# Two-directional Mamba blocks on one core: the output projection one unit later, the eleventh unit's exponentials ahead of a copy, and an earlier load of GpSimd's B

## The chip, the cores and the metric

The kernel runs on one core of one Trainium2 chip. The metric is the device time of one launch in microseconds (us). Three runs of the kernel before gave 26886.77, 26917.85 and 26921.99 us, median 26917.85 us. One further execution was profiled; it took 26881.74 us.

The engines are named as in the profile: PE (TensorE, matmuls), DVE (VectorE), ACT (ScalarE), POOL (GpSimd) and SP (SyncE, which here only issues DMAs, in the order of the program). Every engine works through its own queue in order; between engines there are semaphores.

## The reference, cut to what matters

An image of 64 channels and 128 x 128 pixels is read as sequences, once along its rows and once along its columns. Each sequence goes through a Mamba block forward and backward. A group normalisation and a residual follow, then a block of two 3x3 convolutions with batch normalisation, which is of no concern here.

```python
def mamba(seq, p):                    # seq: (sequences, 128, 64)
    xz = einsum('blc,ec->ble', seq, in_w)
    x, z = xz[..., :128], xz[..., 128:]
    x = silu(causal_conv(x, conv_w, conv_b))          # u
    xdbl = einsum('bld,ed->ble', x, xp_w)
    dt, Bm, Cm = split(xdbl, (4, 16, 16))
    delta = softplus(einsum('blr,dr->bld', dt, dt_w) + dt_b)
    A = -exp(A_log)                                   # (128, 16)
    # scan over tokens t, state h of 128 x 16 for each sequence:
    #   h = exp(delta_t * A) * h + (delta_t * u_t) * B_t ;  y_t = sum_n h * C_t
    y = selective_scan(x, delta, A, Bm, Cm, D)        # + u * D
    y = y * silu(z)
    return einsum('bld,cd->blc', y, out_w)
xr = 0.5 * (mamba(rows) + flip(mamba(flip(rows))))    # the same for columns with other weights
x_rec = 0.5 * (xr + xc); x = silu(group_norm(x_rec)) + x
```

All arithmetic is float32. There are 8 images, 2 orientations, 128 sequences each and 2 directions.

## The kernel before, in words

**Chunks and units.** A chunk `g` is 4 sequences of 128 tokens (512 columns) of one image and one orientation: 32 row chunks and 32 column chunks an image, 512 chunks in all. The scan of a chunk has 128 channels x 16 states x 2 directions; one *unit* is half of the channels (64 channels as 2 x 32) x 4 states of one direction, laid on 128 partitions x 1024 columns. A chunk has 16 units, whose order stands in `ORDER` as (group of 4 states, direction, kind); even units are half 0, odd units half 1.

**What a unit takes.** `decay` makes exp(delta A): two ACT instructions. `drive` multiplies delta u with B: on DVE with B in PSUM (`pb`, made by one matmul in `b_rows` for two units) for kind V, on GpSimd with B loaded by DMA (`bt`, `b_tile`) for kind G. For kind T the product with B is made on tokens: ACT writes `X` = duT * BT in `spread` (four instructions a call, eight calls a chunk), PE turns it in `turn`. `scan` is one DVE instruction, `weigh` one GpSimd multiplication with C (`c`, loaded by DMA in `c_rows`), and `add_up` sums over the states on PE, four units later. In the text a unit's number is written behind the step: `decay(11)`, `drive(13)`, `scan(7)`. Decays of V and G units write the PSUM tile dA0 or dA1, one buffer each, so `decay(k)` waits for the scan two units back that read the same tile.

**The order.** Everything is written out by hand (`tc.manual_schedule`): a loop over `s`, with chunk `n` and unit `r`, issues in each unit the B of later units, the next unit's decay and drive, this unit's scan and weighing, one step of the generator `prepare` for the next chunk, the sums of unit `s - 4`, and DMA issues. `prepare` makes the next chunk's u, delta and their copies during this chunk: a step in each unit. The steps that matter here, as they were:

- r = 8: softplus on ACT (line 307), which needs a table load before it; line 420 loads the exponentials' table back after it.
- r = 9: `bp` (B and C) on PE; `du` = delta u on DVE (326); on ACT the copy `dl` of delta (328) and two small edge copies (330); then `keep(1, du)` and `keep(0, dl)`, 4 DMAs each to a DRAM scratch `dd` (314).
- r = 10: `decay(11)` on ACT, `bc` copy (335) and its DMA to `bd` (337), four transposes `dt` on PE of `du` into the second half of the tile `op` (343), `replicate(g, 0, 0)`: two DMAs of 512 KB that read `dd` back, each row four times, into the next chunk's dl and du for half 0; `add_up(6)`; the DMA c0; at the end of the unit the output projection `emit` of the *previous* chunk into the first half of `op` (487, and 492 for columns).
- r = 11: `b_rows(13)` (409), `turn(12)`, the copy `duT` (347), `replicate(g, 1, 0)` (half 1: `dl10`, `du10`), the DMA `b2` of GpSimd's B, and ACT's copies out of `op` (500 or 505).
- r = 12: `btp` on PE (353). r = 13: its copy `BT` (359), `replicate(g, 1, 1)`, the first `spread`; one further spread in each of the units 14, 15, 0 to 4.
- r = 15 and 0: `drive(0)` and `drive(1)` of the next chunk, which need du of half 0 and `du10`; GpSimd's `drive(2)` needs `b2`.

`dp`, `op`, `btp` and the convolution's `cps` share one PSUM tile (tag `pt`), so each waits until its predecessor was read: `dt` waits for the copy `dl`, which reads delta from `dp`.

Chunks come in three sorts for this text: **row** chunks, where `emit` is one matmul; **normalising** row chunks (the first 16 or so of the following image's), in which one piece of the finished image is normalised in each chunk on ACT, GpSimd and SP; **column** chunks, where `emit` has a second matmul that adds the rows' result, two copies and a `bn_stats`.

Of the kernel before, what the change touches and what calls it, by code (L numbers as in the profile page):

```python
# [46 lines left out]
def tile_mamba2d_then_resblock(ctx: ExitStack, tc: tile.TileContext, x, par, gn, p_w, o_w, new_p, bn, cst, out):  # L47
# [171 lines left out]
    with ExitStack() as st:  # L219
# [54 lines left out]
        def prepare(g, before):  # L274


            w = wt[g["o"]]
            yield
            zp = psa.tile([P, N], F32, name="zp", tag="b")
            nc.tensor.matmul(  # L280
                zp.rearrange("p (q t) -> p q t", t=W), w["wz"], g["xs"][0:C, :, PAD : PAD + W], start=True, stop=True
            )
            yield
            g["sz"] = work.tile([P, N], F32, name="sz", bufs=3)
            nc.scalar.copy(g["sz"], zp)
            cp = psm.tile([P, 2, N], F32, name="cp", tag="pt")
            for d in range(2):
                for k in range(2):
                    t = PAD - 2 * k if d == 0 else PAD + 2 * k + 1
                    nc.tensor.matmul(  # L290
                        cp[:, d, :].rearrange("p (q t) -> p q t", t=W), w["wc"][:, d, k, :],
                        g["xs"][:, :, t : t + W], start=k == 0, stop=k == 1,
                    )
                yield
            yield
            u = work.tile([P, 2, N], F32, name="u")
            nc.scalar.activation(u, cp, AF.Silu, bias=w["conv_b"])  # L297
            if before is not None:
                nc.scalar.activation(before["sz"], before["sz"], AF.Silu)
            g["u"] = u  # L300
            yield
            dp = psm.tile([P, 2, N], F32, name="dp", tag="pt")
            for d in range(2):
                nc.tensor.matmul(dp[:, d, :], w["wd"], u[:, d, :], start=True, stop=True)  # L304
            yield
            yield
            nc.scalar.activation(dp, dp, AF.Softplus, bias=w["dt_b"])
            yield
            dd = g["dd"] = scratch.tile([2, 2, 32, NQ, N], F32, name="dd")

            def keep(k, v):

                for q in range(NQ):
                    nc.sync.dma_start(
                        out=dd[k, :, :, q, :].rearrange("d c t -> c d t"), in_=v[32 * q : 32 * (q + 1)]
                    )


            bp = psa.tile([P, N], F32, name="bp", tag="b")
            for d in range(2):  # L320
                nc.tensor.matmul(
                    bp[2 * NS * d : 2 * NS * (d + 1), :], w["wbc"], u[:, d, :], start=True, stop=True,
                    skip_group_check=True,
                )
            du = work.tile([P, 2, N], F32, name="du", tag="nat")
            nc.vector.tensor_mul(du, dp, u)
            dl = work.tile([P, 2, N], F32, name="dl", tag="nat")
            nc.scalar.copy(dl, dp)  # L328
            for d, edge in enumerate((0, W - 1)):
                nc.scalar.copy(dl[:, d, :].rearrange("p (s t) -> p s t", t=W)[:, :, edge], far)  # L330
            keep(1, du)
            keep(0, dl)
            yield
            bc = work.tile([4 * NS, N], F32, name="bc", tag="tok", bufs=3)
            nc.scalar.copy(bc, bp[0 : 4 * NS, :])
            bd = scratch.tile([2 * NS, 2, N], F32, name="bd")
            nc.sync.dma_start(out=bd.rearrange("n d t -> d n t"), in_=bc)
            g["bd"] = bd

            dt = (shared.pop("pt", None) or psm.tile([P, 2, N], F32, name="dt", tag="pt"))[:, 1, :]  # L340
            for q in range(SEQ):
                c = slice(W * q, W * (q + 1))
                nc.tensor.transpose(dt[:, c], du[:, TD, c], ident)  # L343
            replicate(g, 0, 0)
            yield
            g["duT"] = work.tile([P, SEQ, P], F32, name="duT", bufs=1)
            nc.scalar.copy(g["duT"].rearrange("p q c -> p (q c)"), dt)  # L347
            replicate(g, 1, 0)
            yield

            bt = psm.tile([P, 2, N], F32, name="btp", tag="pt")[:, 0, 0 : 8 * SEQ]
            for q in range(SEQ):
                nc.tensor.matmul(
                    bt[:, 8 * q : 8 * (q + 1)], u[:, TD, W * q : W * (q + 1)], w["wbc"][:, 4 * TG : 4 * TG + 8],
                    start=True, stop=True,
                )
            yield
            g["BT"] = work.tile([P, 8 * SEQ], F32, name="BT", bufs=1)
            nc.scalar.copy(g["BT"], bt)
            replicate(g, 1, 1)  # L360
            yield
            yield
            replicate(g, 0, 1)
            yield

        def spread(g, ng, q):

            t = g["X", ng, q] = work.tile([P, P, 4], F32, name="X", bufs=8)
            for n in range(4):
                k = 8 * q + 4 * (ng - TG) + n  # L370
                nc.scalar.activation(  # L371
                    t[:, :, n], g["duT"][:, q, :], AF.Copy, scale=g["BT"][:, k : k + 1]
                )

        def replicate(g, half, d):

            for k, what in enumerate(("dl", "du")):
                t = rep.tile([P, 2, N], F32, name=what, bufs=5)
                src = g["dd"][k, d, :, 2 * half : 2 * half + 2, :].rearrange("c q t -> c (q t)")
                nc.sync.dma_start(  # L380
                    out=t.rearrange("p q t -> p (q t)"), in_=src.unsqueeze(1).to_broadcast([32, 4, 2 * N])
                )
                g[what, half, d] = t
# [85 lines left out]
        def add_up(g, r):  # L469

            for half in range(2):
                s = g.pop(("s", r + half))
                for j in range(2):
                    q = 2 * half + j
                    nc.tensor.matmul(  # L475
                        g["yp"][32 * q : 32 * (q + 1), :], fold, s[:, j, :], start=False, stop=r == UN - 2,
                        skip_group_check=True,
                    )
# [73 lines left out]
        def conv1(b):  # L552
# [29 lines left out]
        PER = 2 * NCH  # L582
# [4 lines left out]

        EARLY = {3: 4, 4: 7, 11: 12, 12: 15}

        SPREAD = {13: (2, 0), 14: (2, 1), 15: (2, 2), 0: (2, 3), 1: (3, 0), 2: (3, 1), 3: (3, 2), 4: (3, 3)}  # L590

        AHEAD = {15: 3, 0: 3, 7: 3, 8: 3}

        ROWS = {14: 0, 3: 5, 6: 8, 11: 13}

        FETCH = {
            10: ["c0"], 11: ["b2"], 12: ["c2"], 14: ["c4"], 15: ["c5"], 2: ["c8"], 3: ["b10"], 4: ["c10"],
            6: ["c12"], 8: ["c13"],
        }
        blocks, shared = {}, {}  # L600
# [12 lines left out]
        with tc.manual_schedule():  # L613
# [3 lines left out]
                pass  # L617
            for r in (10, 11, 12, 14, 15):
                fetch(gs[0], r)
            for r in (13, 14, 15):  # L620
                spread(gs[0], *SPREAD[r])
            b_rows(*at(0))
            decay(*at(0))
            drive(*at(0))
# [1 line left out]
            for s in range(total + UN):  # L626
# [9 lines left out]
                    if n + 2 < len(gs):  # L636
                        columns(gs[n + 2])
                kind = ORDER[(r + 1) % UN][2]
                if r in ROWS and (g := after if r >= 14 else this):
                    b_rows(g, ROWS[r])  # L640
                if kind == "T" and live:
                    turn(*at(s + 1))
                if kind != "T" and s + 1 < total:
                    decay(*at(s + 1))
                if r in EARLY and live:
                    decay(this, EARLY[r])
# [8 lines left out]
                    gate(prev)  # L655
                if s == total - 1:
                    nc.scalar.activation(this["sz"], this["sz"], AF.Silu)
                if r in CONV and n % PER > 6 or r >= CONV[0] and n % PER == 6:
                    next(conv3, None)
                op = None  # L660
                if r == OUT and (prev or after):
                    op = shared["pt"] = psm.tile([P, 2, N], F32, name="op", tag="pt")
                next(pieces, None)
                if r in SPREAD and (g := after if r >= 13 else this):
                    spread(g, *SPREAD[r])
                if r == LAG and live:
                    skip(this)
                if s % 2 == 0 and LAG <= s < total + LAG:
                    add_up(*at(s - LAG))
                if r in NORM and n % PER:  # L670
                    next(norm, None)
                if g := after if r >= 10 else this:
# [4 lines left out]
                    stack(gs[n + 2], n + 2)  # L677
                if r == 4 and NCH - 6 <= n % PER < PER - 6:
                    load_columns(n // PER, *divmod(n % PER - NCH + 6, 4))
                if r == OUT and prev:  # L680
                    output = emit(prev, op[:, 0, :])
                    next(output)
                elif r == OUT + 1:
                    next(output, None)
                elif r == OUT + 2:
                    next(output, None)
                elif r == OUT + 3 and n % PER == 0 and prev:
                    for _ in conv3:
                        pass
                    norm = normalize(prev["b"], stats.pop(prev["b"]))  # L690
                    next(norm)
                    conv3 = conv1(prev["b"])
# [152 lines left out]
```

## Time and profile before

| | us |
|---|---|
| median of 3 runs | 26917.85 |
| profiled execution | 26881.74 |
| its span (first to last instruction) | 26880.0 |
| first scan at, last scan ends at | 126.2, 25761.4 |
| DVE busy | 23985.6 (89%) |
| GpSimd busy | 23978.1 (89%) |
| ACT busy | 22417.1 (83%) |
| PE busy (matmul) | 19283.9 (72%) |
| mean DMA rate | 171 GB/s |
| granted TensorE clock | 0.839 |

The profiled execution lies 0.13% under the median. The 512 chunks take 25635 us of the span, 50.1 us each; behind them come the second convolution and the last pass. By durations a chunk's 16 scans, 8 drives, `du` and gating are 47.4 us on DVE (neighbours overlap by some 0.08 us each in the records, so about 46 us in sequence); 16 weighings of 2.34 us and 4 drives of 2.36 us are 46.9 us on GpSimd. No engine is busy throughout; the idle time sits at a few places of the chunk.

### The profile page before, as it was taken

How to read it: one execution, taken by the hardware profiler on the slowest of the kernel's cores; microseconds unless marked ns; L12 is line 12 of the kernel's file. 1: busy time of each engine (PE TensorE's matmuls, PEld its weight loads, DVE VectorE, ACT ScalarE, POOL GpSimd, SP SyncE). 2: the span in 40 equal slices, each digit the busy share in tenths (PEclk: the TensorE clock that was granted, in tenths of full speed). 3: DMA queues.
4: the chain of work that ended last, by engine and by line, in shares of the span. 5: the costliest groups of instructions: out<-in, count | busy, mean ns of one | idle time of the engine just before them, and what ended most of it. 6: DMA issues, size and time to landing. Idle time of an engine off the chain costs nothing. (4 is left out here: it accounts for less than half of the span.)

```text
span 26880.0 us, 268089 instructions
## 1 busy us (share of the span) xinstructions
PE 19283.9 (72%) x75308; PEld 7512.1 (28%) x75308; DVE 23985.6 (89%) x14093; ACT 22417.1 (83%) x41390; POOL 23978.1 (89%) x10404
## 2 busy tenths in 40 slices
PE   5667777777777777777776777777777777777776
PEld 2222222222322223222232222222222222322232
DVE  8999999999999999999999999998999999999942
ACT  7888888888888888888888888888888888888842
POOL 7999999999999999999999999999999999999930
PEclk8888888888888888888888888888888888888888
DMA  5555555555555555555555555555555555555545
GB/s 169 172 171 166 162 181 180 167 166 165 186 177 167 170 169 187 171 170 163 173 184 170 166 165 179 180 167 165 165 188 177 164 165 167 189 175 164 163 137 190
DMA packets 2881510, 4604.86 MB, mean 171 GB/s; under 512 B 1055360, under 2 KB 1334032, under 8 KB 2864144
## 3 DMA queue, kind: packets, MB, share of 16 engines
q1 hardware_dynamic: 2859424, 4486.08, 53.8%
q10 hardware_dynamic: 15984, 68.06, 0.9%
q0 software_dynamic: 4608, 33.56, 0.3%
q8 instruction: 601, 9.85, 0.1%
q14 instruction: 893, 7.32, 0.1%
HBM read 3779.98 MB, written 738.98 MB: 168 GB/s over the span
## 5 line engine op out<-in xcount | busy, mean ns | idle before, releaser
L459 POOL TENSOR_TENSOR s<-s,c 128x1024 f32<-128x1024 f32 x8192 | 19143.5, 2368 | 1403.2 <-DVE s L452 868.2
L420 ACT ACTIVATE dA<-dl,A 128x512 f32<-128x512 f32 x12288 | 8487.8, 691 | 1942.5 <-DVE s L452 972.7
L454 DVE TENSOR_TENSOR_SCAN s<-dA,s 128x1024 f32<-128x1024 f32 x4096 | 9195.4, 2275 | 273.0 <-ACT dA L420 236.0
L429 DVE TENSOR_TENSOR s<-du,pb 128x1024 f32<-128x1024 f32 x4096 | 4919.3, 1201 | 1619.8 <-PE pb L409 1294.8
L371 ACT ACTIVATE X<-duT,BT 128x128 f32<-128x128 f32 x16384 | 5612.0, 504 | 16.6
L429 POOL TENSOR_TENSOR s<-du,bt 128x1024 f32<-128x1024 f32 x2048 | 4840.8, 2364 | 420.1 <-DMA bt<-bd 248.6
L475 PE MATMUL yp<-s,fold 128*32 128x512 f32 x32768 | 5016.7, 704 | 13.8 <-POOL s L459 13.5
L452 DVE TENSOR_TENSOR_SCAN s<-s,dA 128x1024 f32<-128x1024 f32 x2048 | 4664.0, 2277 | 1.3 <-PE dA L438 0.7
L452 DVE TENSOR_TENSOR_SCAN s<-dA,s 128x1024 f32<-128x1024 f32 x2048 | 4532.3, 2267 | 8.4 <-POOL s L429 7.0
L409 PE MATMUL pb<-u,wb 128*128 128x512 f32 x4096 | 2570.3, 713 | 1822.9 <-DVE s L429 1381.7
L438 PE MATMUL dA<-ident,X 128*128 128x128 f32 x16384 | 2633.6, 314 | 719.4 <-DVE s L454 701.4
L438 PEld LDWEIGHTS dA<-ident,X 128*128 128x128 f32 x16384 | 2223.8, 163 | 2379.3 <-DVE s L454 1797.1
L420 ACT ACTIVATE s<-dl,A 128x512 f32<-128x512 f32 x4096 | 2706.9, 709 | 9.7
L343 PE MATMUL op<-ident,du 128*128 128x128 f32 x2044 | 569.9, 434 | 2805.1 <-ACT dl L328 2805.1
L290 PE MATMUL cp<-xs,wc 128*128 128x512 f32 x4096 | 2489.0, 739 | 47.9 <-ACT cs L571 47.5
L409 PEld LDWEIGHTS pb<-u,wb 128*128 128x128 f32 x4096 | 737.2, 212 | 3741.0 <-issue 2033.1
L475 PEld LDWEIGHTS yp<-s,fold 128*32 128x32 f32 x32768 | 838.1, 120 | 2727.8 <-issue 1871.0
L304 PE MATMUL dp<-u,wd 128*128 128x512 f32 x2048 | 1287.4, 762 | 324.3 <-ACT u L297 323.8
L280 PE MATMUL zp<-xs,wz 64*128 64x512 f32 x1024 | 657.3, 725 | 1025.1 <-DVE s L429 675.5
L420 ACT ACT_TABLE_LOAD x1030 | 1321.5, 1283 | 18.8
L343 PEld LDWEIGHTS op<-ident,du 128*128 128x128 f32 x2044 | 365.5, 217 | 3268.7 <-ACT dl L328 3268.7
L347 ACT COPY duT<-op 128x512 f32<-128x512 f32 x511 | 299.2, 585 | 1166.1 <-PE op L492 837.2
(118 smaller groups left out, 15013.0 us busy)
## 6 DMA issues: line engine op xcount, KB each, us to landing
dl<-dd SPq DMA_DIRECT2D x2048, 512.0 KB
du<-dd SPq DMA_DIRECT2D x2048, 512.0 KB
c<-bd SPq DMA_DIRECT2D x4096, 256.0 KB
dd<-du SPq DMA_DIRECT2D x2048, 128.0 KB
dd<-dl SPq DMA_DIRECT2D x2048, 128.0 KB
bt<-bd SPq DMA_DIRECT2D x1024, 256.0 KB
xs<-x_h SPq DMA_DIRECT2D x512, 128.0 KB
bd<-bc SPq DMA_DIRECT2D x512, 128.0 KB
```

What stands on the lines that cost most here:

```text
L290: nc.tensor.matmul(cp[:, d, :].rearrange("p (q t) -> p q t", t=W), w["wc"][:, d, k, :], g["xs"][:, :, t : t + W], start=k == 0, stop=k == 1,)
L304: nc.tensor.matmul(dp[:, d, :], w["wd"], u[:, d, :], start=True, stop=True)
L343: nc.tensor.transpose(dt[:, c], du[:, TD, c], ident)
L371: nc.scalar.activation(t[:, :, n], g["duT"][:, q, :], AF.Copy, scale=g["BT"][:, k : k + 1])
L409: nc.tensor.matmul(pb, wt[g["o"]]["wb"][:, P * ng : P * (ng + 1)], g["u"][:, d, :], start=True, stop=True)
L420: nc.scalar.activation(dA[:, j, :], g["dl", half, d][:, j, :], AF.Exp, scale=wt[g["o"]]["A"][:, 2 * half + j, ng : ng + 1])
L429: engine.tensor_mul(s, g["du", half, d], b.unsqueeze(1).to_broadcast([P, 2, N]))
L438: nc.tensor.transpose(dB[:, j, W * q : W * (q + 1)], g["X", ng, q][:, 32 * (2 * half + j) : 32 * (2 * half + j + 1), :].rearrange("p c n - ...
L452: nc.vector.tensor_tensor_scan(s, a, b, 0.0, ALU.mult, ALU.add)
L454: nc.vector.tensor_tensor_scan(s[:, ::-1], a[:, ::-1], b[:, ::-1], 0.0, ALU.mult, ALU.add)
L459: nc.gpsimd.tensor_mul(s, s, c.unsqueeze(1).to_broadcast([P, 2, N]))
L475: nc.tensor.matmul(g["yp"][32 * q : 32 * (q + 1), :], fold, s[:, j, :], start=False, stop=r == UN - 2, skip_group_check=True,)
```

## The change

Five things move; no instruction is added or removed in the steady state.

1. `decay(11)` is issued in `prepare` at r = 9, between `du` and the copy `dl`, no longer at the head of r = 10.
2. `b_rows(13)` is issued at the end of r = 10 behind `add_up(6)`, no longer at the head of r = 11.
3. `emit` runs at the end of r = 11 (behind `turn(12)`), its copies and `bn_stats` one unit later each; normalisation begins at r = 14.
4. `btp` moves from r = 12 to 13 and `BT` from 13 to 14; the spread of r = 13 moves to 14 and that of 14 to 15, which then has two. A step of the first convolution now stands behind the step of `prepare`.
5. The DMA `b2` is issued at r = 10 behind c0, ahead of `dl10` and `du10`.

```diff
             nc.vector.tensor_mul(du, dp, u)
+            if before is not None:
+                decay(before, 11)
             dl = work.tile([P, 2, N], F32, name="dl", tag="nat")
             nc.scalar.copy(dl, dp)
...
             replicate(g, 1, 0)
             yield
-
+            yield
+
+            replicate(g, 1, 1)
             bt = psm.tile([P, 2, N], F32, name="btp", tag="pt")[:, 0, 0 : 8 * SEQ]
...
             nc.scalar.copy(g["BT"], bt)
-            replicate(g, 1, 1)
-            yield
             yield
...
-        SPREAD = {13: (2, 0), 14: (2, 1), 15: (2, 2), 0: (2, 3), 1: (3, 0), 2: (3, 1), 3: (3, 2), 4: (3, 3)}
+        SPREAD = {
+            14: [(2, 0)], 15: [(2, 1), (2, 2)], 0: [(2, 3)], 1: [(3, 0)], 2: [(3, 1)], 3: [(3, 2)], 4: [(3, 3)],
+        }
...
-        ROWS = {14: 0, 3: 5, 6: 8, 11: 13}
+        ROWS = {14: 0, 3: 5, 6: 8, 10: 13}
...
-            10: ["c0"], 11: ["b2"], 12: ["c2"], ...
+            10: ["c0", "b2"], 12: ["c2"], ...
...
-                if r in ROWS and (g := after if r >= 14 else this):
+                if r in ROWS and r != OUT and (g := after if r >= 14 else this):
                     b_rows(g, ROWS[r])
...
-                if kind != "T" and s + 1 < total:
+                if kind != "T" and s + 1 < total and not (r == 10 and after):
                     decay(*at(s + 1))
...
-                if r in CONV and n % PER > 6 or r >= CONV[0] and n % PER == 6:
-                    next(conv3, None)
-                op = None
                 if r == OUT and (prev or after):
                     op = shared["pt"] = psm.tile([P, 2, N], F32, name="op", tag="pt")
                 next(pieces, None)
+                if r in CONV and n % PER > 6 or r >= CONV[0] and n % PER == 6:
+                    next(conv3, None)
...
                     add_up(*at(s - LAG))
+                if r == OUT and live:
+                    b_rows(this, ROWS[r])
...
-                if r == OUT and prev:
+                if r == OUT + 1 and prev:
                     output = emit(prev, op[:, 0, :])
                     next(output)
```

## The prediction

> **What bounds the kernel now.** I read the page first (busy shares and the costliest groups), then the groups by line, then the timeline of a quiet row chunk and of a column chunk on PE, DVE, ACT and SP, and last added the waits up over the whole trace by their place in the chunk. From the page and the groups:
>
> ```profile
> PE 19283.9 (72%) x75308; PEld 7512.1 (28%) x75308; DVE 23985.6 (89%) x14093; ACT 22417.1 (83%) x41390; POOL 23978.1 (89%) x10404
> L343 PE MATMUL op<-ident,du 128*128 128x128 f32 x2044 | 569.9, 434 | 2805.1 <-ACT dl L328 2805.1
> L429 DVE TENSOR_TENSOR s<-du,pb 128x1024 f32<-128x1024 f32 x4096 | 4919.3, 1201 | 1619.8 <-PE pb L409 1294.8 <-PE yp L475 234.4 <-DMA du<-dd 86.6
> ```
>
> DVE's idle time is nearly all at line 429, and 1294.8 us of it ends with a `pb`. By place it is one instruction, `drive(13)`: 3.43 us in each column chunk, 1.62 us in each row chunk. Before it `scan(11)` waits 0.4 to 0.5 us for `decay(11)`. The timeline says why (a column chunk, PE; a row chunk, DVE and ACT):
>
> ```profile
> 2150.10 1.11 PE L343 MATMUL op<-ident,du 128*128 128x128 f32 x4 [5.49 <-ACT dl L328]
> 2151.14 1.94 PE L475 MATMUL yp<-s,fold 128*32 128x512 f32 x8
> 2153.01 2.08 PE L487 MATMUL op<-y,wo 128*128 128x512 f32 x2
> 2154.88 1.90 PE L492 MATMUL op<-xp,ident 128*128 128x512 f32 x2
> 2156.61 1.04 PE L409 MATMUL pb<-u,wb 128*128 128x512 f32 x2
> ...
> 1313.13 1.42 ACT L420 ACTIVATE dA<-dl,A 128x512 f32<-128x512 f32 x2
> 1314.61 1.01 ACT L328 COPY dl<-dp 128x1024 f32<-128x1024 f32 x1
> 1317.36 2.29 DVE L454 TENSOR_TENSOR_SCAN s<-dA,s 128x1024 f32<-128x1024 f32 x1 [0.42 <-ACT dA L420]
> 1320.97 1.22 DVE L429 TENSOR_TENSOR s<-du,pb 128x1024 f32<-128x1024 f32 x1 [1.32 <-PE pb L409]
> ```
>
> The chain is softplus, `decay(10)`, copy `dl`, transposes, `add_up(6)`, `emit`, `pb`, `drive(13)`. I count from the end of `scan(7)`, t = 0. There softplus ends at 3.85 in every sort of chunk, since `decay(9)` waits for t = 0. Averages over the trace, column / row / normalising row: `dl` ends 8.31 / 7.82 / 7.85, `drive(13)` starts 15.85 / 13.48 / 13.51, `drive(1)` of the next chunk 28.32 / 25.82 / 26.44, the next `scan(7)` ends 50.97 / 48.65 / 49.55. In half of the column chunks and a fifth of the rows `drive(9)` has waited up to 1.27 us for PE ("late" below); there `dl` ends at 8.93 in columns, else at 7.65.
>
> **The change part by part.**
>
> *`decay(11)` ahead of `dl`.* Table load 1.28 and `decay(10)` 1.42 after softplus end at 6.56. Now `decay(11)` follows (1.42; its scan 9 ended at 5.49), to 7.98, and `dl` ends at 9.00, 1.35 later than 7.65; in late chunks at 9.25, since ACT idled there for `du` anyway. `scan(11)` no longer waits (needed at 8.8).
>
> *`emit` behind `pb` and `turn(12)`.* On PE it took 1.33 us of the chain in rows (2153 to 2156.6, 3.5 us, in columns). What is left is `dl`, transposes, sums, `pb`. This very sequence is in the trace once, in the first chunk, which has no `emit`:
>
> ```profile
> 158.61 1.12 PE L343 MATMUL op<-ident,du 128*128 128x128 f32 x4 [5.49 <-ACT dl L328]
> 159.66 1.94 PE L475 MATMUL yp<-s,fold 128*32 128x512 f32 x8
> 161.53 1.46 PE L409 MATMUL pb<-u,wb 128*128 128x512 f32 x2
> ```
>
> From 158.61 to 162.99 is 4.38 us. So `pb` ends at 9.05 + 4.38 = 13.43 and `drive(13)` starts at 13.45, late chunks 13.75. Rows hardly move (13.28 before in the undisturbed ones: +0.2; late ones -0.5); columns gain 1.7, late ones 2.7. Note `pb`: 1.46 us, against 1.04 behind `emit`. PE comes to this chain after 5.5 us of idleness and doubles its pace some 4 us into it, so `emit` warmed it up for `pb`. The Trainium skill (TensorE: Matmul & The Clock Gate, Part 1: The HAM clock gate) has the rule: half rate after an idle window of about 3.4 us, full rate only after as long a busy one. By that rule alone both passes of `pb` could run slow, and up to 0.4 us a chunk, 200 us in all, would be lost of the gain. The one row shows the first pass at 0.86 us and the second fast. My bound for it is 1.04 to 1.9 us, two passes at the 0.95 of a slow `emit` pass; I take 1.46.
>
> *`emit`'s new place.* In columns PE ends `turn(12)` (0.87) at 14.3, `emit` at 17.8 if slow, the two copies (1.25) at 19.05, then `decay(14)` at 20.45; `scan(14)` is due at 20.45, behind `scan(13)` and the `bn_stats`. Nothing is lost, but with no margin: each us more would show in full. `duT` no longer waits for `emit` (3.4 us in columns), which costs and brings nothing while ACT is ahead. `btp`, `BT` and the convolution's step come a unit later; `drive(0)` at 22 is the first to need what queues behind them on PE.
>
> *Two spreads at r = 15.* 1.2 us of ACT go from ahead of `decay(0)`, where ACT idles 1.3 to 1.6 us, to behind it. It idles 0.4 + 1.1 us in rows and 0.2 + 0.6 in columns before `decay(1)` and `decay(2)`, then 0.43 in columns before `decay(9)`. So it is covered; uncovered it would cost 1.2 us a chunk.
>
> *SP.* Here comes what is late next. The queue issues in order, in the row chunk:
>
> ```profile
> 1316.44 2.63 SPq L314 DMA_DIRECT2D dd<-dl  x4
> 1319.17 0.57 SPq L337 DMA_DIRECT2D bd<-bc  x1
> 1320.60 0.53 SPq L380 DMA_DIRECT2D dl<-dd  x1
> 1321.18 0.60 SPq L380 DMA_DIRECT2D du<-dd  x1
> 1324.88 0.51 SPq L394 DMA_DIRECT2D c<-bd  x1
> 1325.50 0.55 SPq L380 DMA_DIRECT2D dl<-dd  x1
> 1326.09 0.60 SPq L380 DMA_DIRECT2D du<-dd  x1
> 1326.74 0.60 SPq L402 DMA_DIRECT2D bt<-bd  x1
> ```
>
> The last du is `du10`. By the landing records it lands at 24.52 in undisturbed rows (25.36 in late ones, 25.83 in normalising ones, 24.59 and 25.90 in columns), and `drive(1)` could start at 25.5: one us of slack in rows, none in normalising ones, which already wait 0.7 us for it on average, as here:
>
> ```profile
> 13067.29 1.22 DVE L429 TENSOR_TENSOR s<-du,pb 128x1024 f32<-128x1024 f32 x1 [1.55 <-DMA du<-dd]
> ```
>
> Everything from `keep(0, dl)` on follows `dl`. It was issued at 8.5, held by the four issues for du until 8.44 rather than by `dl`; now at 9.4: 0.9 later, 0.4 in late rows, nothing in late columns (9.75 both ways) and nearly nothing in normalising rows (9.44 now, held by a store that waits for GpSimd). `b2` ahead of `du10` costs its issue, 0.60 us; the bounds are 0 (the DMA engines are 63 to 88% busy in those us of that chunk) and 1.23 (256 KB at the pace of `dl10`, which lands 2.46 us after c0). I take 0.6, the row nearest. The Trainium skill (DMA: Bandwidth & Descriptors, Queues, rings and completion order) has each ring served in order. By that, `du10` would land where `b2` lands now, 0.74 us later, and the sum below would be 70 us smaller; yet packets of both run side by side here. GpSimd's own wait for `b2` (248.6 us in all) ends, but GpSimd has about 2 us a chunk to spare.
>
> So `drive(1)` starts at the later of readiness and landing. Row: 24.52 + 0.9 + 0.6 = 26.02, start 26.06 (ready 25.7); late row 26.4; with 108 and 27 chunks the mean is 26.13, +0.31 on 25.82. Normalising row: 26.54, +0.1. Column: 24.59 + 1.5 = 26.09, start 26.13 (ready 26.0), late 26.54; mean 26.35, -1.97. From `drive(1)` to the next `scan(7)` DVE's sequence is unchanged (22.7 to 23.1 us).
>
> Sum: 239 x (-1.97) = -471; 135 x 0.31 = +42; 128 x 0.1 = +13; the 8 chunks at an image's start -2 each, as columns, -16: together -432 us. The profiled time 26881.7 becomes 26450, and on the median (0.13% above it) 26485.
>
> **Rivals.** (a) *The transfer stays hidden*: `b2` fits into idle DMA slots and `du10` moves only with `dl`. Then rows start `drive(1)` when ready (about 25.76 on average), normalising rows at 25.9, columns at 26.0 and 26.3: -8, -64, -516, -20, or -608 us, 26310 on the median. For it: the idle share of the DMA engines then. Against: SP's issue alone costs 0.6. (b) *PE cold and DMA in order*: `pb` 0.4 us slower and `b2` at its full 1.23, 0.63 us on each of 502 chunks: +316, leaving -116, 26800. For it: the slow first passes. Against: the first chunk's row. (c) *Slower*: the delta path becomes the bound. If `dl`'s 1.35 goes through to the keeps in full and `b2` costs 1.23, `du10` lands 2.6 later in rows: `drive(1)` +1.6, +1.3 in normalising rows, +0.5 in late rows, and columns gain only 0.4 and 1.45: 173 + 166 + 14 - 46 - 180 = +127 us, 27045. It turns slower from about 2.35 us of delay on. For it: normalising rows wait for this DMA already. Against: SP's own issues held the keeps.
>
> **How the numbers follow.** My forecast has 0.55, (a) 0.15, (b) 0.15, (c) 0.15. No change within 0.2% (54 us, about what a measurement of this kernel can tell) is the edge of (b) and gets 0.05. Faster is 0.55 + 0.15 + 0.10 = 0.80, slower 0.15. The range runs from (a) to just past (b), 26300 to 26830, and leaves (c) out.
>
> **What would show it.** Right: `scan(11)` without a wait; `drive(13)` at 13.4 to 13.8 in every sort of chunk, so row and column chunks nearly equally long, about 49; `duT` without a wait on `op`; a new wait of DVE at `drive(1)` for du, some 0.4 us a chunk in rows. Wrong: `drive(1)` waiting over 1 us for du in most chunks; `pb` over 1.5 us; `scan(14)` waiting for `decay(14)`; GpSimd still waiting for `b2`.

## The result and the profile after

The changed kernel takes 26730.3 us (median of 4 runs, 26705.95 to 26760.29); the kernel before, on the same chip, 26902.3 us (4 runs, 26881.61 to 26921.99). The ratio is 0.9937, 95% interval 0.9919 to 0.9954. It is faster by 0.6%, and inside the range, but by 172 us where 432 were forecast. The profiled execution took 26705.95 us (span 26704.2), 176 under that of before.

The page after, at the lines shown of before (the lines of the code have moved by two):

```profile
PE 19008.3 (71%) x75308; PEld 7246.5 (27%) x75308; DVE 23980.8 (90%) x14093; ACT 22216.9 (83%) x41390; POOL 24011.8 (90%) x10404
...
L456 DVE TENSOR_TENSOR_SCAN s<-dA,s 128x1024 f32<-128x1024 f32 x4096 | 9163.0, 2273 | 39.6 <-ACT dA L422 8.5
...
L345 PE MATMUL op<-ident,du 128*128 128x128 f32 x2044 | 569.5, 434 | 3368.1 <-ACT dl L330 3368.1
```

DVE's waits after, by the line that waited and by what it waited for (us in total, times, longest us):

```profile
DVE s L431 <- PE pb L411: 1215.1, 517, 2.8
...
DVE s L431 <- DMA du<-dd: 333.2, 298, 13.1
```

and before:

```profile
DVE s L429 <- PE pb L409: 1294.8, 515, 3.6
...
DVE s L454 <- ACT dA L420: 236.0, 504, 0.9
DVE s L429 <- PE yp L475: 234.4, 230, 1.7
...
DVE s L429 <- DMA du<-dd: 86.6, 71, 12.9
```

The wait of `scan(11)` for an exponential is gone (8.5 us are left on `dA`, against 236.0), and `drive(13)` still waits for `pb`, but now alike in all chunks. The wait for `du` has grown from 86.6 to 333.2 us, in 298 waits against 71. By place, counted from the end of `scan(7)` and averaged over the trace (before, then after):

| | column | row | normalising row |
|---|---|---|---|
| `dl` ends | 8.31, 8.88 | 7.82, 8.88 | 7.85, 8.94 |
| first `keep(0, dl)` issued | 9.14, 9.25 | 8.66, 9.26 | 9.47, 9.31 |
| `drive(13)` starts | 15.85, 13.63 | 13.48, 13.65 | 13.51, 13.71 |
| `du10` issued | 18.79, 19.44 | 18.21, 19.41 | 19.31, 19.42 |
| `du10` lands | 25.27, 26.51 | 24.69, 26.59 | 25.86, 26.62 |
| ready for `drive(1)` but for du10 | 28.40, 26.26 | 25.71, 25.95 | 25.75, 26.02 |
| `drive(1)` starts | 28.32, 26.81 | 25.82, 26.82 | 26.44, 26.89 |
| next `scan(7)` ends | 50.97, 49.47 | 48.65, 49.67 | 49.55, 49.98 |

(Neighbours overlap by some 0.08 us in the records, so a start can stand just ahead of its readiness. The sorts go by place in the image: of the 135 rows 8 run a column's `emit`, and of the 128 normalising rows the 16 of the first image have nothing to normalise; without these 16 that column changes by 0.2 us at most.)

All three sorts have become one. By the last row 239 x (-1.50) + 135 x 1.02 + 128 x 0.43 = -166 us; the 8 chunks at image starts and the rest of the span give the other 10. A row chunk, its own timeline on ACT, PE and DVE (`scan(7)` ends at 1337.03):

```profile
1342.92 2.02 ACT L422 ACTIVATE dA<-dl,A 128x512 f32<-128x512 f32 x3
1344.88 1.00 ACT L330 COPY dl<-dp 128x1024 f32<-128x1024 f32 x1
...
1345.94 1.11 PE L345 MATMUL op<-ident,du 128*128 128x128 f32 x4 [6.69 <-ACT dl L330]
1346.98 1.94 PE L477 MATMUL yp<-s,fold 128*32 128x512 f32 x8
1348.84 2.08 PE L411 MATMUL pb<-u,wb 128*128 128x512 f32 x2
1350.71 1.26 PE L440 MATMUL dA<-ident,X 128*128 128x128 f32 x8
1351.81 1.02 PE L489 MATMUL op<-y,wo 128*128 128x512 f32 x2
...
1350.96 1.22 DVE L431 TENSOR_TENSOR s<-du,pb 128x1024 f32<-128x1024 f32 x1 [2.78 <-PE pb L411]
...
1364.62 1.22 DVE L431 TENSOR_TENSOR s<-du,pb 128x1024 f32<-128x1024 f32 x1 [1.45 <-DMA du<-dd]
```

The chain is `dl`, transposes, sums, `pb` as forecast, and `emit` stands behind it. Two things differ from the forecast: `pb` takes 2.08 us, both passes slow (the granted clock over it is 0.50), and `drive(1)` waits 1.45 us for `du10`.

SP's queue in the same chunk:

```profile
1348.92 0.53 SPq L382 DMA_DIRECT2D dl<-dd  x1
1349.51 0.59 SPq L382 DMA_DIRECT2D du<-dd  x1
1354.54 0.51 SPq L396 DMA_DIRECT2D c<-bd  x1
1355.10 0.60 SPq L404 DMA_DIRECT2D bt<-bd  x1
1355.80 0.54 SPq L382 DMA_DIRECT2D dl<-dd  x1
1356.40 0.60 SPq L382 DMA_DIRECT2D du<-dd  x1
```

SP issues the pair for half 0 and then nothing from 1350.10 to 1354.54: the next in its queue is c0, which reads `bd`, and `bd` has not landed. The pair with `du10`, which needs nothing of `bd`, stands behind that wait and now behind `b2` too. Over the whole trace (waits of SP's queue):

```profile
SPq L396 <- DMA bd<-bc: 2020.7, 511, 4.9
```

That is 3.95 us in each chunk.

### The profile page after: what moved, and what is told of

The parts are those of the page before. It is cut to its first block, busy times and chain, and to the rows that moved or that the text cites. A ratio compares the mean times of both kernels' runs of the same rounds, so it can differ in the third digit from the quotient of the medians.

```text
span 26704.2 us, 267388 instructions
## 1 busy us (share of the span) xinstructions
PE 19008.3 (71%) x75308; PEld 7246.5 (27%) x75308; DVE 23980.8 (90%) x14093; ACT 22216.9 (83%) x41390; POOL 24011.8 (90%) x10404
## 5 line engine op out<-in xcount | busy, mean ns | idle before, releaser
L431 DVE TENSOR_TENSOR s<-du,pb 128x1024 f32<-128x1024 f32 x4096 | 4923.0, 1202 | 1662.4 <-PE pb L411 1215.1
L440 PE MATMUL dA<-ident,X 128*128 128x128 f32 x16384 | 2467.7, 300 | 783.1 <-DVE s L456 777.4
L440 PEld LDWEIGHTS dA<-ident,X 128*128 128x128 f32 x16384 | 2115.2, 157 | 2352.7 <-DVE s L456 1608.8
L290 PE MATMUL cp<-xs,wc 128*128 128x512 f32 x4096 | 2652.6, 782 | 78.4 <-ACT cs L573 78.0
L280 PE MATMUL zp<-xs,wz 64*128 64x512 f32 x1024 | 874.2, 947 | 1530.4 <-DVE s L431 1108.2
L304 PE MATMUL dp<-u,wd 128*128 128x512 f32 x2048 | 1115.1, 671 | 339.5 <-ACT u L297 339.0
L290 PEld LDWEIGHTS cp<-xs,wc 128*128 128x128 f32 x4096 | 890.6, 241 | 1435.0 <-issue 908.9
```

Of the source, the lines that this page charges most:

```text
L290: nc.tensor.matmul(cp[:, d, :].rearrange("p (q t) -> p q t", t=W), w["wc"][:, d, k, :], g["xs"][:, :, t : t + W], start=k == 0, stop=k == 1,)
L431: engine.tensor_mul(s, g["du", half, d], b.unsqueeze(1).to_broadcast([P, 2, N]))
L440: nc.tensor.transpose(dB[:, j, W * q : W * (q + 1)], g["X", ng, q][:, 32 * (2 * half + j) : 32 * (2 * half + j + 1), :].rearrange("p c n - ...
```

## The experiments

All medians are of 4 runs; the ratios are to the kernel before on the same chip, with 95% intervals. That kernel took 26898 to 26912 us beside the experiments, so a step from one run to another of a different chip is good to some 15 us. Theory: the move of the projection pays fully, and the two small edits beside it, `decay(11)` ahead of `dl` (part 1) and `b2` ahead of `du10` (part 5), give it back through `du10`. Rival: the gain went to a `pb` that PE runs slowly.

**e1: the changed kernel without part 5.**

```diff
-            10: ["c0", "b2"], 12: ["c2"], ...
+            10: ["c0"], 11: ["b2"], 12: ["c2"], ...
```

> The changed kernel with the load of b2 back at r = 11, behind dl10 and du10; all else as changed. Theory (the landing of du10 ends drive(1)'s wait, and b2 ahead of it costs 0.66 us of issue and as much again of transfer): du10 lands 1.3 us earlier, at about 25.2 us behind scan(7) in place of 26.5; drive(1) starts when it is ready, about 26.0 to 26.1 in place of 26.8; 0.7 us on some 500 chunks, about 26380 us, DVE's waits for du under 60 us in all (333 now), GpSimd waiting again for b2, about 1 us a chunk, at no cost. Rival A (b2 is harmless and du10 is late only because delta's copy is): du10 lands within 0.3 us of 26.5, 26700 us. Rival B (GpSimd's wait for b2 comes back and costs what it did): no gain or a loss, 26700 to 26900 us.

Measured: 26435.5 us, ratio 0.9826 (0.9812 to 0.9841); 295 us less than the changed kernel. `du10` is issued at 18.75 instead of 19.44 in columns and lands at 25.28, in rows at 25.28 too: 1.23 and 1.31 us earlier. The wait for it falls to a third (120.2 us; under 60 were expected), and GpSimd's for `b2` is back, at no cost that columns and rows show:

```profile
DVE s L431 <- DMA du<-dd: 120.2, 120, 13.0
...
POOL s L431 <- DMA bt<-bd: 540.9, 380, 4.4
```

In normalising rows it has a cost. A store of the normalised image stands ahead of the keeps in SP's queue and waits for GpSimd: it is issued at 6.5 instead of 5.3, the keeps of `dl` at 9.7 instead of 9.3, and `du10` lands only 0.47 us earlier there.

`pb` and with it `drive(13)`'s wait stays (1155.0 us against 1215.1), so the rival does not explain these 295 us.

**e2: the changed kernel without part 1** (`decay(11)` back at the head of r = 10).

```diff
             nc.vector.tensor_mul(du, dp, u)
-            if before is not None:
-                decay(before, 11)
...
-                if kind != "T" and s + 1 < total and not (r == 10 and after):
+                if kind != "T" and s + 1 < total:
```

> The changed kernel with decay(11) back at the head of r = 10, behind delta's copy; all else as changed. Theory (the copy sets both the matmul chain to drive(13) and the keeps): the copy ends at 7.65 us behind scan(7) in place of 8.86, drive(13) starts at 12.1 to 12.4 in place of 13.6, scan(11) waits 0.4 us again, but du10 lands only 0.6 earlier, at about 25.9, so that drive(1), ready at 24.6, waits over 1 us for it: 0.75 us a chunk, about 26330 us, DVE waiting for du some 600 us in all. Rival A (drive(13) is all that counts): 1.4 us a chunk, 26000 us. Rival B (the wait of scan(11) that part 1 removed is worth its 0.45 us a chunk): slower than the changed kernel, 26950 us.

Measured: 26445.7 us, ratio 0.983 (0.9816 to 0.9845); 285 us less than the changed kernel, 116 more than expected. `drive(13)` starts at 12.5 to 12.6, readiness is 1.1 us earlier, and most of that turns into a wait for `du10`, which lands at 26.0 to 26.3:

```profile
DVE s L429 <- DMA du<-dd: 602.4, 424, 13.0
...
DVE s L429 <- PE pb L409: 374.1, 496, 1.1
DVE s L454 <- ACT dA L420: 227.4, 538, 0.9
```

Against the changed kernel the wait for `pb` fell by 841 us (1215.1 to 374.1), that for `du` rose by 269 and that of `scan(11)` came back with 219 (227.4 less 8.5 for the exponentials' tile after). That leaves 353, of which 270 show at the end of the span. So part 1 removes a wait of 0.4 us at `scan(11)` and puts 1.1 us on the chain to `drive(13)`.

**e3: both undone**, only the projection, `b_rows(13)` and the spreads moved.

> Both of the above: only the output projection, B on tokens and the spreads are moved, and pb of drive(13) stands ahead of the projection. Theory: drive(13) at 12.1 to 12.4, du10 at about 24.5, drive(1) at 24.6 to 24.9 in place of 26.8, 1.9 us a chunk; GpSimd's 46.9 us and a wait of 0.8 us for b2 come close to the new length of a chunk, about 47.7 us; 25800 us. Rival A (b2's load harmless): as with delta's copy first alone, about 26330 us. Rival B (GpSimd's wait for b2 now shows in full): 48.3 us a chunk, 26100 us.

Measured: 26070.4 us, ratio 0.9689 (0.9674 to 0.9703): 660 us less than the changed kernel. `drive(13)` starts at 12.5 to 12.7 and `drive(1)` at 25.2 in columns and rows, but at 26.15 in normalising rows, where the keeps of `dl` are issued only at 9.58, behind the same store as in e1, and `du10` lands at 25.93. Normalising rows end 1.2 to 1.3 us behind the others, some 160 us over 128 chunks, and that is the larger part of what the expectation missed.

**e5 and e6: the kernel before with part 5 alone, and with part 1 alone.**

```diff
-            10: ["c0"], 11: ["b2"], 12: ["c2"], ...
+            10: ["c0", "b2"], 12: ["c2"], ...
```

> The kernel before with part 5 alone: b2 loaded at r = 10 behind c0, ahead of dl10 and du10. Theory (1.25 us on du10's landing): no change in column chunks, where drive(1) is ready at 28.4 and du10 would land at 26.5; in rows du10 lands at 25.95 and in normalising rows at 27.1, 0.3 to 0.8 us behind readiness; about 0.4 us on 135 and 0.7 us on 128 chunks, 140 us, about 27040 us. Rival (GpSimd's end of waiting for b2 is worth more): 248 us of waits gone, 26700 us.

```diff
             nc.vector.tensor_mul(du, dp, u)
+            if before is not None:
+                decay(before, 11)
...
-                if kind != "T" and s + 1 < total:
+                if kind != "T" and s + 1 < total and not (r == 10 and after):
```

> The kernel before with part 1 alone: decay(11) ahead of delta's copy; the projection stays in front of pb. Theory: the copy ends 1.2 us later where ACT did not idle for du (all but some 180 chunks), and 0.3 us later in the others; transposes, sums, projection and pb follow; scan(11)'s wait goes but is swallowed. drive(13) at 14.5 in rows and 16.4 in columns in place of 13.28 and 15.15: 1.2 us on some 320 chunks and 0.3 us on 180, 440 us, about 27340 us. Rival (what the edit is meant for: DVE's 240 us of waits at scan(11) end): 26660 us.

Measured: e5 27045.8 us, ratio 1.0055 (1.004 to 1.007); e6 27275.5 us, ratio 1.014 (1.0123 to 1.0157). Each is a loss by itself. In e5 `du10` lands 1.28 us later in columns and 1.55 in rows; columns, which had 3 us of slack before `drive(1)`, end as before (50.97), and rows pay 0.83. In e6 the chain through `pb` pays:

```profile
DVE s L431 <- PE pb L411: 2133.3, 512, 5.3
```

With the wait of `scan(11)` (236.0 us) gone, `drive(13)` starts at 14.75 instead of 13.48 in rows. The factors add up nearly, with the projection moved: part 1 costs 365 us (e1 - e3), part 5 375 (e2 - e3), both 660.

**e4: a second transfer ahead.** The changed kernel with c2 also ahead of `dl10` and `du10`.

```diff
-            10: ["c0", "b2"], 12: ["c2"], ...
+            10: ["c0", "b2", "c2"], ...
```

> The changed kernel with a second load of the same size, c2, issued at r = 10 behind b2, ahead of dl10 and du10 too: the suspected cost doubled. Theory: du10 lands another 1.3 us later, at 27.8, and drive(1) starts 1.2 us later; 600 us in all, 27330 us; DVE's wait for du about 900 us. Rival A (a load there is harmless): 26730 us. Rival B (only the issue counts): 0.65 us a chunk, 27050 us.

Measured: 27072.7 us, ratio 1.0061 (1.0044 to 1.0078), 342 us more than the changed kernel, or 0.68 on each of 502 chunks. `du10` is issued 0.68 to 0.77 us later and lands 0.9 us later in columns and 0.8 in rows and normalising rows. The waits:

```profile
DVE s L431 <- PE pb L411: 1227.6, 517, 2.8
DVE s L431 <- DMA du<-dd: 646.6, 420, 12.9
```

`pb`'s part has not changed; only the wait for `du` has. What reached the end is near the issue alone, not the issue and as much transfer again: the second 256 KB costs less than the first.

**e7 and e8: `du10` out from behind the wait.** Its pair is issued right behind that for half 0, ahead of c0 and of its wait for `bd`; e7 on e2, e8 on the changed kernel. `b2` stays ahead of nothing that DVE waits for.

```diff
             replicate(g, 0, 0)
+            replicate(g, 1, 0)
...
-            replicate(g, 1, 0)
             yield
```

> As delta's copy first, and dl10 and du10 are issued at r = 10 right behind the DMAs of half 0, ahead of c0, so that they no longer queue behind SP's wait for bd nor behind b2; b2 follows c0. Theory: du10 lands near 22 to 23, drive(1) starts when ready, about 25.0; b2 lands by about 24, before GpSimd gets to it; chunks of about 47.8 us, normalising ones 48.5, 25880 us. Rival A (c0 or b2, now last, become what is waited for): no better than with both put back, 26070 us. Rival B (GpSimd's 46.9 us of work and its place in the chunk are the bound already): 26000 us.

> The changed kernel, with dl10 and du10 issued at r = 10 ahead of c0, and b2 behind c0. Theory (in the changed kernel the landing of du10 is the only thing between drive(1) and its readiness at 26.0): drive(13) stays at 13.6, no wait of DVE for du, 48.7 us a chunk, 26330 us. Rival (the DMA engines are the limit, not the order of the queue): du10 lands as late as before or c0 is late, 26650 us or more.

Measured: e7 25876.35 us, ratio 0.962 (0.9606 to 0.9635), the fastest of all; e8 26291.1 us, ratio 0.9774 (0.9759 to 0.9788). SP's queue in e7, a row chunk:

```profile
1305.62 0.53 SPq L380 DMA_DIRECT2D dl<-dd  x1
1306.20 0.71 SPq L380 DMA_DIRECT2D du<-dd  x1
1307.08 0.65 SPq L380 DMA_DIRECT2D dl<-dd  x1
1307.78 0.60 SPq L380 DMA_DIRECT2D du<-dd  x1
1311.15 0.51 SPq L394 DMA_DIRECT2D c<-bd  x1
1311.70 0.60 SPq L402 DMA_DIRECT2D bt<-bd  x1
```

`du10` lands at 22.2 to 23.3 and `b2` still at 23.6 to 24.7. DVE's waits for `du` are down to 12, one of them 12.9 of the 20.6 us:

```profile
DVE s L429 <- PE pb L409: 472.6, 509, 1.1
...
DVE s L429 <- DMA du<-dd: 20.6, 12, 12.9
```

The whole step from the changed kernel to e8, 439 us, is what `du10` cost there. The step from e8 to e7, 415 us, is part 1's price with no DMA in the way.

**e9: the sums behind `pb`.** e7 with `add_up(6)` moved from r = 10 to r = 11, behind `pb` and `turn(12)`, to shorten the chain once more.

```diff
-                if s % 2 == 0 and LAG <= s < total + LAG:
-                    add_up(*at(s - LAG))
+                if (s % 2 == 0 and r != OUT or r == OUT + 1) and LAG <= s - s % 2 < total + LAG:
+                    add_up(*at(s - s % 2 - LAG))
```

> As the version with delta's copy first and du10 early, and add_up(6) moved from r = 10 to r = 11, behind pb and turn(12). Theory (in that version the matmuls between delta's copy and drive(13) are what is left: 1.04 us of transposes, 1.87 of sums, 1.8 of pb at PE's slow pace): pb now waits for the bc copy, which ends at 9.8, and ends at 11.6; drive(13) at 11.7 in place of 12.7, no wait there; chunks of about 47.0 us, then held by GpSimd's 46.9, normalising ones 48.2; 25550 us. Rival A (the sums were not in the way, or PE is still slow at turn(12), so that scan(12) waits as long): 25880 us. Rival B (GpSimd's work is already the bound at 47.8): 25850 us.

Measured: 27093.0 us, ratio 1.0069 (1.0053 to 1.0086), 1217 us more than e7. A column chunk on PE and DVE:

```profile
2211.63 2.08 PE L409 MATMUL pb<-u,wb 128*128 128x512 f32 x2 [1.03 <-ACT bc L335]
2213.50 1.92 PE L438 MATMUL dA<-ident,X 128*128 128x128 f32 x8
2215.34 1.94 PE L475 MATMUL yp<-s,fold 128*32 128x512 f32 x8
...
2217.31 1.22 DVE L429 TENSOR_TENSOR s<-du,pb 128x1024 f32<-128x1024 f32 x1 [3.85 <-PE yp L475]
```

and DVE's waits over the trace:

```profile
DVE s L429 <- PE yp L475: 1755.6, 592, 3.9
```

`pb` ends on average at 12.00 instead of 12.71, as meant, and `drive(13)` starts at 15.11 instead of 12.69 in columns. What it waits for now is the end of the sums. The likely reason is a buffer: `drive` writes a tile of `s`, of which there are 8 (the pool `unit`), and the sums are the last to read one and so free it. This is read from the code, since of what `drive(13)` reads and writes (`du`, `pb`, `s`) the sums touch `s` alone; no run changed the number of tiles. The theory that they lay on the path only because PE took them ahead of `pb` has fallen: they are on it in their own right.

## Why the prediction was right or wrong

Two steps failed: the price of `b2` ahead of `du10`, taken at half of what it is, and the start of `drive(1)`, put at the later of two averages. The chain to `drive(13)`, the main mechanism, came as forecast.

**The chain to `drive(13)`: right.** `dl` ends at 8.88 in columns and rows (9.00 forecast), the wait of `scan(11)` is gone, `drive(13)` starts at 13.63 to 13.71 in all three sorts (13.45, late 13.75). `emit` at its new place costs nothing: it takes 1.02 us in rows and 2.73 in columns there, less than the 3.5 us I had allowed, and `scan(14)` does not wait for `decay(14)`. The two spreads and the later `btp` cost nothing either; `duT` no longer waits; GpSimd no longer waits for `b2`. Late column chunks fell from 124 of 239 to 23.

**`pb`: the value taken too low.** 1.46 us was taken from one row, 1.04 to 1.9 as the bound. It takes 1.76 on average and over 1.7 in 64% of the chunks, two slow passes; single ones reach 2.08, past the bound. The chain from the transposes to its end is 4.67 us instead of 4.38, and that is the 0.2 to 0.3 by which readiness came later than forecast (25.95 against 25.7 in rows, 26.26 against 26.0 in columns). The first chunk's PE had been idle for 5.49 us, the changed kernel's is for 6.69, but that is not the cause: in e3, with 5.49, `pb` takes 1.83. The granted clock shows what is. It returns from 0.5 to 1.0 between 2.8 and 6.2 us after the first transpose, on average after 4.5 us in both kernels; `pb` now begins 2.9 us after it, before 6.4 us in columns, and the clock granted over `pb` went from 0.97 to 0.64 on average. In the first chunk, the forecast's one row, the clock happened to return in the middle of `pb`, at 162.23. The Trainium skill (TensorE: Matmul & The Clock Gate, Part 1: The HAM clock gate) has full rate only after a busy window as long as the idle one, 3.4 us. Here the window before `pb` is 2.9 us of transposes and sums (1345.94 to 1348.84 above), and the trace agrees in most chunks: both passes run slow in 64% of them. What this cost in time no run isolates; on average `du10` comes later still (26.51 against 26.26 in columns).

**`b2` ahead of `du10`: the step that was mis-sized.** I took its issue alone, 0.60 us, out of 0 to 1.23. It cost 1.23 us of `du10`'s landing in columns and 1.31 in rows (e1 against the changed kernel): 0.69 us of issue, and the time from issue to landing went from 6.53 to 7.07 us. In normalising rows it cost 0.47, since there `du10` was issued no later (19.58 and 19.42). The upper bound was the value. In the sum this step carried 175 us (26485 less the 26310 of rival (a), where `b2` costs nothing); in the runs it is 295. The 120 us between them are about half of the 245 by which the median came out above the forecast. My reason for the low value, DMA engines 63 to 88% busy, holds for the first part of the transfer only. In the chunk it was read from, `du10` was issued at 1326.09 and landed at 1332.70; the engines were 80% busy from 1326 to 1330 and 100% from 1330 to 1332.5, so that `b2` had no idle time to go into there. The Trainium skill (DMA: Bandwidth & Descriptors, Queues, rings and completion order) has the descriptors of a ring consumed in order, from which I had estimated 0.74 us; the trace agrees in the sign and puts it at 1.23 to 1.31, beyond that.

**The keeps: slightly too late.** The first `keep(0, dl)` in undisturbed rows moved from 8.5 to 9.2, not to 9.4: 0.7, where 0.9 was taken. Together, 0.65 too little for `b2` and 0.2 too much here make the 0.47 us by which `du10` in undisturbed rows lands at 26.49 instead of 26.02.

**The later of two times: left out.** I set `drive(1)` at the later of two averages. Both fluctuate: `du10`'s landing spreads from 24.6 to 29.6 in columns, readiness from 25.5 to 27.2. Their averages are 26.51 and 26.26, but `drive(1)` starts on average at 26.81. In undisturbed rows 26.73 against 26.53 (26.49 and 0.04 of start): 0.2 us in each chunk. Of the 0.67 us by which `drive(1)` there is later than forecast (26.73 against 26.06), 0.47 are the landing and 0.20 this. Over all chunks `drive(1)` came 0.46 later than forecast in columns, 0.69 in rows and 0.35 in normalising rows: 110 + 93 + 45 = 248 us, which is the miss (256 us on the profiled time). Some 130 of them are the later landing and some 115 this.

**From `drive(1)` to the next `scan(7)`: right.** 22.66 us in columns, 22.85 in rows, 23.09 in normalising rows (22.7 to 23.1).

**The rivals.** (a), a transfer that stays hidden, is out: e1 shows it costing 295 us. (b), PE cold and the DMA in order, saw both: `pb` slow and `b2` at its full price. Its 26800 is nearer to the result than 26485, in part by luck: it charged each of 502 chunks with 0.63 us for the landing, where the whole miss was 0.51 and only half of that the landing. (c) named the right wait, but `dl`'s 1.35 us did not go through in full.

## What to carry to other kernels

Before moving a copy or a transfer "for free", list what stands in the same in-order queue behind it and behind each wait in that queue: here two small edits gave back 660 of 832 us (26902 to 26070 in e3), and one pair of DMAs issued ahead of another's wait took 439 us off the changed kernel. Where a step begins at the later of two times that fluctuate, put their spread into the sum; the later of the averages is too early. An instruction on the critical path may be there because its end frees a buffer, and not because of its place in the order (so it seems in e9): ask what its end releases, not only what stands behind it.

## What the runs showed of the hardware that was not expected

- A transfer of 256 KB put ahead of a pair of 512 KB each in one queue delayed the landing of the second of the pair, `du10`, by 1.23 to 1.31 us (that of the first, `dl10`, by 1.7), 0.69 us of it by issue and 0.54 to 0.61 by a longer time from issue to landing (6.53 to 7.07 us in columns, 6.57 to 7.18 in rows). A second one (e4) cost 0.7 more at `drive(1)`.
- With the pair issued before c0 and `b2` (e7), `du10` is under way for 8.5 us in columns (13.74 to 22.23) instead of 6.5 and still lands 3 us earlier than in e1. `b2` lands 1.4 us behind it and nobody waits long: 49.2 us for `bt` in all on GpSimd.
- `emit` in columns takes 2.73 us behind `pb` and 3.67 ahead of it, in rows 1.02 and 1.66: PE's granted clock is back at 1.0 later in the burst. The cost went to `pb` instead, 1.08 us before and 1.76 after. The chain to `pb`'s end still became 1.8 us shorter (6.47 to 4.67).
